# Gram blocks in groups of 32 tokens, two blocks in a row: a correlation stage beside attention

## The chip, the cores and the metric

The kernel runs on one NeuronCore of a Trainium2 chip. The metric is the device time of one execution in microseconds (us); the time given for a kernel is the median of three runs. One further execution is profiled, and everything that is read from a trace comes from that one.

The core has TensorE (PE, matrix products into PSUM; PEld is its weight loads), VectorE (DVE), ScalarE (ACT), GpSimd (POOL) and SyncE (SP), whose queue issues nearly all DMAs here. Each works through its own instructions in order and waits on semaphores for the others.

## The reference

The input is a batch of 8 images of 768 channels and 32 x 32 pixels. Two layers are computed in float32, with a group normalisation over 32 groups of channels ahead of each:

```python
x = x + _L0_conv_ref(_gn(x), L0_conv_W_qkv, L0_conv_W_proj, L0_conv_b_proj)
x = x + _L1_conv_ref(_gn(x), L1_conv_conv_w, L1_conv_conv_b)
```

The first layer is an attention over the 1024 pixels (tokens) with 12 heads of 64, whose scores come from the variances of keys and values alone:

```python
var_v = jnp.var(v, axis=-1, ddof=1, keepdims=True)
var_k = jnp.var(k, axis=-1, ddof=1, keepdims=True)
scores = var_v @ jnp.swapaxes(var_k, -2, -1) * scale
attn = jax.nn.softmax(scores, axis=-1)
out = attn @ v
```

Its result goes through a 768 x 768 projection. The second layer normalises every pixel's channel vector to length 1 and correlates it with 28 of its neighbours in a 7 x 7 window (the two diagonals, the middle column and the middle row), then mixes the 768 channels and the 28 correlations with a 1 x 1 convolution:

```python
norm = jnp.sqrt(jnp.sum(feature * feature, axis=1, keepdims=True))
feat_n = feature / jnp.maximum(norm, EPS)
feat_pad = jnp.pad(feat_n, ((0, 0), (0, 0), (PAD, PAD), (PAD, PAD)))
corr = jnp.stack([jnp.sum(feat_pad[:, :, r:h + r, cc:w + cc] * feat_n, axis=1) for r, cc in _offsets()], axis=1)
x = jnp.concatenate([feature, corr], axis=1)
out = jnp.einsum('bchw,oc->bohw', x, conv_w) + conv_b[None, :, None, None]
```

## The kernel before

**Layout.** Channels lie on the 128 partitions, six to each (`J = 6`), so an image is a tile of 128 x 6 x 1024. The large products (keys and values, projection, convolution) are done with Strassen's seven products; all of them have 64 columns of weights per matmul, two matmuls side by side in the two halves of the array (`halves`, L346 to L350). A float32 matmul stands in the trace as two records, one for each of its passes.

**Stages.** For image b a round of the main loop runs the keys and values of pairs 3 to 5 (half 1), the attention of its six pairs of heads (`Attention`, `Pair`), beside it the second layer's convolution of image b-1 (`Conv`), then the projection, then the keys and values of pairs 0 to 2 of image b+1. The work order is fixed when the program is built: a planner (`Clock`) holds a planned time, every unit of TensorE work advances it by a cost written down as a constant (`KV_US`, `T_US`, `STEP_US`, `GRAM_US`), and jobs for other engines are put behind it with `later.after(us, job)`, or `later.after_dve(us, job)`, which counts from the planned end of VectorE's work. These times only set the order of the instructions in each engine's queue; on the chip semaphores decide.

**The correlation of an image** (`Corr`). Only products of a pixel with pixels at up to 3 rows below and 3 columns to either side are needed. The 1024 tokens are cut into 8 blocks of four image rows (128 tokens). For each block t:

- `turn` (L1128) copies the block's tokens on GpSimd (ScalarE in the last image) so that the tokens of the left 16 columns come first and those of the right 16 after, two operations of 128 x 384 each, into the one buffer of `turnpool`.
- `gram` (L1143) multiplies, for each of the six channel chunks and for each side, the 64 tokens of that side (weights) with the part of the image they need: 7 rows (the block's four and three more) by 19 columns, 133 in all; the last block has 4 rows, 76. The two sides go to the two halves of the partitions in one PSUM tile of the pool `smp`, whose two banks are shared with other small products.
- `out` copies the result to one of three `wins` buffers (VectorE; ScalarE in the last image) and writes it with two DMAs to a DRAM area `windowed`, with a pitch between tokens such that a later read finds fixed neighbours at fixed places. After blocks 3 and 7 comes `diagonals` (L1182), which reads the 20 wanted products of each token of four blocks with four DMAs. `scale` (L1198) makes the inverse lengths (`rn`, a power on GpSimd) and multiplies; `to_dram` turns them into rows by two small matmuls (`ct`) and writes them to DRAM; after the second half `gather` (L1231) reads the rows into `cs` (u) and a tile of `uvpool` (v), each shifted by its offset, VectorE multiplies the two, and three DMAs copy `cs` to the other three quarters of the partitions. The convolution's units then add the correlations with one more matmul from `cs` (`join`, L1058).

**What places the Gram.** `work_off` (L1403) runs the attention's steps (four key tiles, 6.9 us) whenever their exponentials are made, and otherwise the next unit of the list `rest`. Gram units lie in a list of their own, `beside`: `next_to` (L1396) takes one of them before and after each attention step, and at two or three fixed places in `rest`; `remaining` takes what is left before the convolution starts. The first `turn` of an image is made when the keys and values of the next half are nearly done (`start_corr`); for image 0 it is made right after the normalisation (`turn_first`), and `"turned"` is released 6 us later.

**Other places that the change touches.** `KeysValues.unit` (L644) ends a half with `spread`, which reduces the variances, takes a maximum over partitions on GpSimd (`partition_all_reduce`, L714) and writes the rows that the attention reads. `make_sums` (L631) forms on GpSimd the token sums that the Strassen products of keys and values need. At the start `keep_warm` runs matmuls on an identity while the first data arrive.

Of the kernel before, what the change touches and what calls it, by code (L numbers as in the profile page):

```python
# [13 lines left out]
P = 128  # L14
# [15 lines left out]
TALL, WIDE = MT // 2 + 3, HW + 3  # L30
AHEAD_OF = [o for first, _, count in RUNS for o in range(first, first + count)][1:]
# [25 lines left out]
GRAM_US = 1.4  # L57
WARM, BRIDGE = 38, (3, 6)
# [33 lines left out]
class Clock:  # L92


    def __init__(self):
        self.now, self.count, self.jobs = 0.0, 0, []
        self.act, self.rows, self.poll = 0.0, ([], []), lambda: None
        self.dve = 0.0
# [74 lines left out]
def two_layers(ctx, tc, x, wkv, wproj, bproj, wconv, wcorr, bconv, out):  # L173
# [17 lines left out]
    turnpool = pool("turnpool", 1)  # L191
    wk = pool("wk", 3)
    uvpool = pool("uvpool", 1)
# [259 lines left out]
    wins = [const.tile([P, WIN], F32, name=f"win{i}") for i in range(3)]  # L453
# [141 lines left out]
    class KeysValues:  # L595
# [48 lines left out]
        def unit(self, half, d, n, g, p):  # L644
# [18 lines left out]
            if d == 1 and n == len(PAIR) - 1:  # L663
                self.over = half == 1
                more = 4.0 if half and not b else 0.0
# [458 lines left out]
    class Corr:  # L1124
# [17 lines left out]

        def gram(self, t):  # L1143

            b = self.b
            tall = min(TALL, H - 4 * t)
# [5 lines left out]
            for j in range(J):  # L1152
                image = self.f[:, j, :].rearrange("p (y x) -> p y x", x=W)
                for side in range(2):
                    left = side * (HW - 3)
                    nc.tensor.matmul(  # L1156
                        ps[side * HD : (side + 1) * HD, :n].rearrange("p (y x) -> p y x", x=WIDE),
                        lhsT=block[:, j, side, :],
                        rhs=image[:, 4 * t : 4 * t + tall, left : left + WIDE],
                        start=j == 0, stop=j == J - 1,  # L1160
                    )
            for ahead in range(t + 1, min(t + (3 if b == NB - 1 else 2), MT)):
# [3 lines left out]
            def out():  # L1166
                win = wins[t % 2 if t < MT - 1 else 2]
# [4 lines left out]
                for side in range(2):  # L1172
                    to = windowed[b % 2][t : t + 1, side * (HD * PITCH + HD - 3) :]
                    nc.sync.dma_start(
                        out=windows(to, (HW * PITCH - 3, 4), (PITCH, HW), (1, WIN)), in_=win[side * HD : (side + 1) * HD, :]
# [4 lines left out]
            later.after(GRAM_US + 0.25, out)  # L1180

        def diagonals(self, hf):  # L1182
# [13 lines left out]
            later.after(6.0, lambda: self.scale(hf, dd))  # L1196

        def scale(self, hf, dd):  # L1198
# [7 lines left out]
            def columns():  # L1206
# [4 lines left out]
                later.after_dve(0.7 if b else 5.0 if hf else 7.5, lambda: to_dram(dn))  # L1211
# [19 lines left out]
        def gather(self):  # L1231
# [3 lines left out]
            v = uvpool.tile([NCH, N], F32, tag="uv", name=f"v{b}")  # L1235
            nc.sync.dma_start(out=v[NS:NCH, :], in_=windows(r[0:1, PAD:], (0, NS + 4), (1, N)))
            nc.sync.dma_start(out=u[2 * NS : NCH, :], in_=windows(r[1:2, PAD:], (0, 4), (1, N)))
            for n, (first, apart) in enumerate(PICKED):
                k, row = 3 * n, 2 + AHEAD_OF.index(first)
                nc.sync.dma_start(out=u[k : k + 3, :], in_=windows(r[row : row + 1, PAD:], (apart * ROW, 3), (1, N)))  # L1240
                nc.sync.dma_start(out=v[k : k + 3, :], in_=windows(r[0:1, PAD + first :], (apart, 3), (1, N)))
# [150 lines left out]
    def remaining(beside):  # L1392
        while beside:
            next_to(beside)
# [250 lines left out]
```

## Time and profile before

| | us |
|---|---|
| median of three runs | 2574.16 |
| lowest and highest run | 2573.71, 2581.83 |
| profiled execution | 2576.79 |
| its span, first to last instruction | 2575.1 |
| TensorE's records of Gram, first seven images (L1156): 133 columns, 76 columns | 84.3, 8.2 |
| the same in the last image | 10.0, 1.0 |
| GpSimd's turned blocks (L1141), 112 operations | 110.7 |
| granted TensorE clock | 1.000 |

A line of a profile page gives an engine, the line of the code, the operation, the tiles it writes and reads and how often; times are in us unless marked ns. A record's busy time is not its cost: matmuls overlap their neighbours, so the cost of a group of them is the time from its first start to the first start of what follows. A timeline's columns are start, duration (to the end of the last one merged), engine, line, operation, output and inputs, shapes and count; in brackets stands the engine's idle time before, and what ended it. A line of the list of waits has the waiting engine, tile and line, what it waited for, the time in all, how often, and the longest one.

### The profile page before, as it was taken

To read this page: it belongs to the slowest core of one execution; us is meant where nothing else is said; L and a number is where in the kernel's file an instruction comes from. 1 tells how busy PE (TensorE), PEld (TensorE's weight loads), DVE (VectorE), ACT (ScalarE), POOL (GpSimd) and SP (SyncE) were. 2 spreads that over 40 slices of the span, in tenths; PEclk is the share of its full clock that TensorE was granted. 3 is DMA by queue.
4 is the path that set the end of the run, shared out by engine and by line. 5 is a ranking of instruction groups with operands and counts; after the bars stand their busy time and mean duration, and the time that the engine had idled before them with its cause. 6 is when DMAs were issued, how large, how long until landed. Compare 5 with 4: busy or idle time off the path is not lost.

```text
span 2575.1 us, 40595 instructions
## 1 busy us (share of the span) xinstructions
PE 2566.3 (100%) x14694; PEld 1246.2 (48%) x14694; DVE 1582.3 (61%) x4125; ACT 1417.5 (55%) x1972; POOL 422.4 (16%) x449
## 2 busy tenths in 40 slices
PE   9999999999999999999999999999999999999999
PEld 6545356334554347633476434664344333475333
DVE  6868735775447853478534785358853587535764
ACT  1497279811697217971179711897118971199610
POOL 4320130004300043000430003300133001331000
PEclk9999999999999999999999999999999999999999
DMA  8766366355563655636556365563655636445333
GB/s 293 293 220 229 102 212 186 120 198 170 185 190 116 198 168 178 205 98 206 169 176 202 97 212 169 168 204 100 218 166 174 207 107 218 151 158 167 119 109 109
DMA packets 331818, 448.56 MB, mean 174 GB/s; under 512 B 68431, under 2 KB 252623, under 8 KB 331619
## 3 DMA queue, kind: packets, MB, share of 16 engines
q1 hardware_dynamic: 329554, 442.62, 53.8%
q10 hardware_dynamic: 2064, 3.34, 0.4%
q8 instruction: 117, 1.92, 0.3%
q14 instruction: 83, 0.67, 0.1%
HBM read 376.70 MB, written 64.78 MB: 171 GB/s over the span
## 4 chain that ended last, share of the span: by engine, by line
PE 96%; DMA 2%; ACT 1%; DVE 1%; SPq 0%; issue 0%; POOL 0%; ACTq 0%; POOLq 0%; DVEq 0%
PE x L350 34%; PE av L801 25%; PE y L350 17%; PE z L350 10%; PE own L350 5%; PE gr L1156 3%; PE den L832 1%; ACT ex L775 1%; ACT junk L785 0%; DMA bk<-kdr 0%; DMA kv<-in_wkv_dram 0%; PE z L1062 0%; PE cc L1275 0%; PE y L1062 0%; DVE acc L167 0%
## 5 line engine op out<-in xcount | busy, mean ns | idle before, releaser
L775 ACT ACTIVATE ex<-bc,nk 128x1024 f32<-128x1024 f32 x768 | 826.9, 1139 | 382.4 <-DMA bc<-vdr 256.7
L801 PE MATMUL av<-ex,v 128*64 128x512 f32 x3072 | 699.8, 593 | 0.3 <-ACT ex L775 0.2
L801 PEld LDWEIGHTS av<-ex,v 128*64 128x64 f32 x3072 | 303.8, 137 | 355.3 <-issue 262.0
L785 ACT ACTIVATE junk<-bk,vm 128x1024 bf16<-128x1024 f32 x368 | 421.4, 1145 | 41.5 <-issue 17.8
L167 DVE TENSOR_TENSOR acc<-acc,ex 128x1024 f32<-128x1024 f32 x300 | 344.7, 1216 | 0.0
L350 PE MATMUL y<-kv,s 128*64 128x384 f32 x1488 | 265.6, 487 | 0.9 <-POOL s L636 0.9
L350 PE MATMUL x<-kv,xn 128*64 128x384 f32 x1512 | 261.4, 486 | 0.3 <-DMA kv<-in_wkv_dram 0.3
L350 PE MATMUL x<-kv,s 128*64 128x384 f32 x1488 | 256.2, 486 | 0.0
L229 ACT COPY kp<-x 128x384 f32<-128x384 f32 x28 | 13.4, 479 | 404.8 <-PE x L350 396.0
L350 PEld LDWEIGHTS x<-kv,xn 128*64 128x64 f32 x1512 | 134.2, 137 | 109.9 <-issue 83.9
L350 PEld LDWEIGHTS x<-kv,s 128*64 128x64 f32 x1488 | 131.6, 137 | 108.0 <-issue 87.1
L350 PEld LDWEIGHTS y<-kv,s 128*64 128x64 f32 x1488 | 130.1, 137 | 99.6 <-issue 75.3
L530 POOL TENSOR_TENSOR rstda<-vea,neghalf 128x1 f32<-128x1 f32 x8 | 4.8, 596 | 949.1 <-DVE vea L167 949.1
L1141 POOL TENSOR_TENSOR turn<-f,ones 128x384 f32<-128x384 f32 x112 | 110.7, 1010 | 242.1 <-PE gr L1156 182.2
L350 PE MATMUL z<-kv,xn 128*64 128x384 f32 x768 | 135.4, 486 | 0.0
L350 PE MATMUL x<-f,wt 128*64 128x512 f32 x504 | 120.0, 593 | 0.0
L167 DVE TENSOR_TENSOR v<-y,v 128x128 f32<-128x128 f32 x180 | 41.0, 283 | 124.1 <-PE y L350 124.1
L636 POOL TENSOR_TENSOR s<-xn 128x384 f32<-128x384 f32 x64 | 65.6, 1035 | 294.8 <-PE x L350 183.0
L167 DVE BATCH_NORM_STATS2 vbn<-v 128x6 f32<-128x64 f32 x720 | 101.7, 211 | 0.0
L167 DVE SCALAR_TENSOR_TENSOR xn<-x,bconv_sb,xn 128x512 f32<-128x512 f32 x63 | 46.5, 747 | 89.1 <-PE x L350 86.1
L229 ACT COPY acc<-li 32x256 f32<-32x256 f32 x128 | 51.6, 403 | 82.9 <-DVE li L167 81.5
L350 PEld LDWEIGHTS z<-kv,xn 128*64 128x64 f32 x768 | 72.6, 137 | 49.9 <-issue 36.0
(199 smaller groups left out, 3126.2 us busy)
## 6 DMA issues: line engine op xcount, KB each, us to landing
kv<-kvs SPq DMA_DIRECT2D x124, 576.0 KB
kv<-in_wkv_dram SPq DMA_DIRECT2D x95, 576.0 KB
bc<-vdr SPq DMA_DIRECT2D x96, 512.0 KB
f<-in_x_dram SPq DMA_DIRECT2D x48, 512.0 KB
bk<-kdr SPq DMA_DIRECT2D x46, 512.0 KB
x1d<-f SPq DMA_DIRECT2D x42, 512.0 KB
xn<-x1d SPq DMA_DIRECT2D x42, 512.0 KB
out_dram<-xn SPq DMA_DIRECT2D x82, 256.0 KB
```

Source lines behind the costliest of these rows:

```text
L167: return getattr(self.engine, name)(*args, **kw)
L229: nc.scalar.copy(to, at)
L350: nc.tensor.matmul(out[at], lhsT=lhsT[:, at], rhs=rhs, start=start, stop=stop, **kw)
L530: nc.gpsimd.tensor_tensor(self.rstd, ve, neghalf[:, 0:1], ALU.pow)
L636: nc.gpsimd.tensor_tensor(self.sums[g][:, 0], a[g][2], a[g][3], ALU.add)
L775: nc.scalar.activation(ex, self.bc[e], AF.Exp, scale=self.kv.nk[self.half][:, h, t : t + 1])
L785: nc.scalar.activation(junk, self.bk[e], AF.Exp, scale=self.kv.m2[self.half][:, h, t : t + 1], accum_out=self.sums[:, e, t : t + 1],)
L801: nc.tensor.matmul(self.av[hf][e * HD : (e + 1) * HD, :], lhsT=self.vt[:, t, e, :], rhs=exs[e][:, hf * HF : (hf + 1) * HF], start=t == 0, ...
L832: nc.tensor.matmul(den[at * 32 : (at + 1) * 32, :], lhsT=ones[:, 0:32], rhs=self.acc[e][:, hf * HF : (hf + 1) * HF], start=True, stop=True,)
L1141: nc.gpsimd.tensor_tensor(to[:, :, side], half, windows(ones, ones.ap[0], (0, J), (HW, 4), (1, HW)), ALU.mult)
L1156: nc.tensor.matmul(ps[side * HD : (side + 1) * HD, :n].rearrange("p (y x) -> p y x", x=WIDE), lhsT=block[:, j, side, :], rhs=image[:, 4 * ...
```

## The change

For all images but the last, each side's 64 tokens are divided into two groups of two image rows, so a block has four groups of 32 tokens. Each group is multiplied with five rows by 19 columns (95), or four rows in the last block (76), and goes to a quarter of the partitions. The windows of a block are written with four DMAs of 32 partitions (two in the last block). `grams` runs two blocks in a row and stands in `beside` in the place of `gram`; another pair is taken 5.8 us of planned time later at the earliest, but for `remaining`, which sets that aside. `turnpool` has two buffers, `turn` is made for two blocks ahead (two at the start of an image), and `v` of `gather` lies in two tiles of that pool in the place of `uvpool`. There are four `wins` buffers instead of three. The scaling of the diagonals is expected 13 us after their reads are issued instead of 6, and the rows' transposition at other times. The spread of image 0's half 1 is put 8 us later. Image 0's pairs of blocks have more places in `rest`, and `"turned"` is released 8 us after the first turned blocks. Four more matmuls stand in the first stretch of `keep_warm` and one more in a later one. The last image keeps two groups and single blocks.

```diff
--- before.py
+++ after.py
@@ -28,6 +28,7 @@
 RUNS = ((0, 0, 4), (31, -1, 3), (62, -2, 5), (93, -3, 7))
 HW = W // 2
 TALL, WIDE = MT // 2 + 3, HW + 3
+SHORT = 2 + 3
 AHEAD_OF = [o for first, _, count in RUNS for o in range(first, first + count)][1:]
 NA = len(AHEAD_OF)
 PAD = 99
@@ -54,8 +55,8 @@
 TAIL = 0.0
 EXP, SUM, STEP_US = 1.07, 1.15, 1.73
 KV_US, T_US, CORR_US = 1.93, 2.58, 1.2
-GRAM_US = 1.4
-WARM, BRIDGE = 38, (3, 6)
+GRAM_US, TURN_US = (1.3, 2.4), 3.4
+WARM, BRIDGE = 42, (3, 7)
 
 
 
@@ -95,7 +96,7 @@
     def __init__(self):
         self.now, self.count, self.jobs = 0.0, 0, []
         self.act, self.rows, self.poll = 0.0, ([], []), lambda: None
-        self.dve = 0.0
+        self.dve = self.turned = 0.0
 
     def after(self, us, job):
         self.count += 1
@@ -188,9 +189,8 @@
     bcpool = pool("bcpool", 4)
     bkpool = pool("bkpool", 2)
     expool = pool("expool", 2 * AHEAD)
-    turnpool = pool("turnpool", 1)
+    turnpool = pool("turnpool", 2)
     wk = pool("wk", 3)
-    uvpool = pool("uvpool", 1)
     st = pool("st", 1)
     xbank = pool("xbank", 2, space=PSUM)
     ybank = pool("ybank", 2, space=PSUM)
@@ -450,7 +450,7 @@
 
     rows = [dconst.tile([NROW, ROW], F32, name=f"rows{i}") for i in range(2)]
     windowed = [dconst.tile([MT, P * (PITCH + 2)], F32, name=f"windowed{i}") for i in range(2)]
-    wins = [const.tile([P, WIN], F32, name=f"win{i}") for i in range(3)]
+    wins = [const.tile([P, WIN], F32, name=f"win{i}") for i in range(4)]
     for win in wins:
         nc.gpsimd.memset(win, 0.0)
     across = const.tile([W, NA], F32, name="across")
@@ -662,7 +662,7 @@
                 kv_stream.done((b, half, d, p))
             if d == 1 and n == len(PAIR) - 1:
                 self.over = half == 1
-                more = 4.0 if half and not b else 0.0
+                more = 12.0 if half and not b else 0.0
                 later.after(KV_US + 0.5 + more, lambda: later.after_dve(0.0, lambda: self.spread(half)))
 
         def stats(self, kind, half, t, src):
@@ -1140,10 +1140,18 @@
                     half = rows[:, :, :, side, :]
                     nc.gpsimd.tensor_tensor(to[:, :, side], half, windows(ones, ones.ap[0], (0, J), (HW, 4), (1, HW)), ALU.mult)
 
+        def grams(self, t):
+
+            clock.turned = clock.now + GRAM_US[1] + TURN_US
+            for n in range(2):
+                self.gram(t + n)
+
         def gram(self, t):
 
             b = self.b
-            tall = min(TALL, H - 4 * t)
+            last = t == MT - 1
+            groups = 2 if b == NB - 1 else 4
+            tall = min(SHORT if groups == 4 else TALL, H - 4 * t)
             n = tall * WIDE
             if t not in self.turned:
                 self.turn(t)
@@ -1151,33 +1159,39 @@
             ps = other([P, SPAN], f"gr{b}_{t}")
             for j in range(J):
                 image = self.f[:, j, :].rearrange("p (y x) -> p y x", x=W)
-                for side in range(2):
-                    left = side * (HW - 3)
+                each = P // groups
+                for at in range(groups):
+                    side, low = divmod(at, groups // 2)
+                    left, first = side * (HW - 3), 4 * t + (0 if last else 2 * low)
                     nc.tensor.matmul(
-                        ps[side * HD : (side + 1) * HD, :n].rearrange("p (y x) -> p y x", x=WIDE),
-                        lhsT=block[:, j, side, :],
-                        rhs=image[:, 4 * t : 4 * t + tall, left : left + WIDE],
+                        ps[at * each : (at + 1) * each, :n].rearrange("p (y x) -> p y x", x=WIDE),
+                        lhsT=block[:, j, side, low * each : (low + 1) * each],
+                        rhs=image[:, first : first + tall, left : left + WIDE],
                         start=j == 0, stop=j == J - 1,
                     )
-            for ahead in range(t + 1, min(t + (3 if b == NB - 1 else 2), MT)):
+            for ahead in range(t + 1, min(t + 3, MT)):
                 if ahead not in self.turned:
                     self.turn(ahead)
 
             def out():
-                win = wins[t % 2 if t < MT - 1 else 2]
+                win = wins[t % 3 if t < MT - 1 else 3]
                 if b < NB - 1:
                     vector.tensor_copy(win[:, :n], ps[:, :n])
                 else:
                     act_copy(0.3, win[:, :n], ps[:, :n])
-                for side in range(2):
-                    to = windowed[b % 2][t : t + 1, side * (HD * PITCH + HD - 3) :]
+                whole = last or groups == 2
+                size, count, down = (WIN, 4, 0) if whole else (SHORT * WIDE + 3, 2, 2 * (HW * PITCH - 3 + WIDE))
+                for first in range(0, P, count * HW):
+                    side, low = divmod(first, HD)
+                    to = windowed[b % 2][t : t + 1, side * (HD * PITCH + HD - 3) + (down if low else 0) :]
                     nc.sync.dma_start(
-                        out=windows(to, (HW * PITCH - 3, 4), (PITCH, HW), (1, WIN)), in_=win[side * HD : (side + 1) * HD, :]
+                        out=windows(to, (HW * PITCH - 3, count), (PITCH, HW), (1, size)),
+                        in_=win[first : first + count * HW, :size],
                     )
                 if t % 4 == 3:
                     later.after(4.0, lambda: self.diagonals(t // 4))
 
-            later.after(GRAM_US + 0.25, out)
+            later.after(1.65 if b == NB - 1 else GRAM_US[t % 2] + 0.25, out)
 
         def diagonals(self, hf):
 
@@ -1193,7 +1207,7 @@
                     ),
                 )
                 at += count
-            later.after(6.0, lambda: self.scale(hf, dd))
+            later.after(13.0 if b < NB - 1 else 6.0, lambda: self.scale(hf, dd))
 
         def scale(self, hf, dd):
 
@@ -1208,7 +1222,7 @@
                 vector.tensor_copy(dn[:, :, 0], rn)
                 for q in range(4):
                     vector.scalar_tensor_tensor(dn[:, q, 1:NROW], dd[:, q, :], rn[:, q : q + 1], mask, ALU.mult, ALU.mult)
-                later.after_dve(0.7 if b else 5.0 if hf else 7.5, lambda: to_dram(dn))
+                later.after_dve(0.7 if b == NB - 1 else (5.0 if hf else 7.0) if b else 3.0 if hf else 6.0, lambda: to_dram(dn))
 
             def to_dram(dn):
                 pt = small(f"ct{b}_{hf}")
@@ -1232,20 +1246,23 @@
 
             b, r = self.b, rows[self.b % 2]
             u = cs.rearrange("p a n -> p (a n)")[0:NCH, 0:N]
-            v = uvpool.tile([NCH, N], F32, tag="uv", name=f"v{b}")
-            nc.sync.dma_start(out=v[NS:NCH, :], in_=windows(r[0:1, PAD:], (0, NS + 4), (1, N)))
+            vs = [turnpool.tile([P, J * P], F32, tag="turn", name=f"v{b}_{hf}") for hf in range(2)]
+            for hf, v in enumerate(vs):
+                nc.sync.dma_start(out=v[NS:NCH, :HF], in_=windows(r[0:1, PAD + hf * HF :], (0, NS + 4), (1, HF)))
             nc.sync.dma_start(out=u[2 * NS : NCH, :], in_=windows(r[1:2, PAD:], (0, 4), (1, N)))
             for n, (first, apart) in enumerate(PICKED):
                 k, row = 3 * n, 2 + AHEAD_OF.index(first)
                 nc.sync.dma_start(out=u[k : k + 3, :], in_=windows(r[row : row + 1, PAD:], (apart * ROW, 3), (1, N)))
-                nc.sync.dma_start(out=v[k : k + 3, :], in_=windows(r[0:1, PAD + first :], (apart, 3), (1, N)))
+                for hf, v in enumerate(vs):
+                    nc.sync.dma_start(out=v[k : k + 3, :HF], in_=windows(r[0:1, PAD + first + hf * HF :], (apart, 3), (1, HF)))
                 nc.sync.dma_start(
                     out=u[NS + k : NS + k + 3, :],
                     in_=windows(r[row : row + 1, PAD - first :], (apart * (ROW - 1), 3), (1, N)),
                 )
 
             def product():
-                vector.tensor_tensor(u, u, v, ALU.mult)
+                for hf, v in enumerate(vs):
+                    vector.tensor_tensor(cs[0:NCH, hf, :], cs[0:NCH, hf, :], v[0:NCH, :HF], ALU.mult)
                 vector.tensor_tensor(cs[0:NCH, 2, :], cs[0:NCH, 0, :], cs[0:NCH, 1, :], ALU.subtract)
                 for n in range(1, 4):
                     nc.sync.dma_start(out=cs[n * FOUR : n * FOUR + NCH, :, :], in_=cs[0:NCH, :, :])
@@ -1391,11 +1408,12 @@
 
     def remaining(beside):
         while beside:
+            clock.turned = 0.0
             next_to(beside)
 
     def next_to(beside):
 
-        if beside and ready.issuperset(beside[0][1]):
+        if beside and ready.issuperset(beside[0][1]) and clock.now >= clock.turned:
             us, _, unit = beside.pop(0)
             unit()
             clock.pass_time(us)
@@ -1421,7 +1439,7 @@
 
     def turn_first():
         start_corr(0)
-        later.after(6.0, lambda: ready.add("turned"))
+        later.after(8.0, lambda: ready.add("turned"))
 
     def project(b, ots, held=None):
         f = first_f[0] if b == 0 else layer1[b - 1][0]
@@ -1538,6 +1556,7 @@
     def start_corr(b):
         corrs.append(Corr(b, layer1[b][0]))
         corrs[-1].turn(0)
+        corrs[-1].turn(1)
 
     second, corrs = [], []
     later.after(26.0, lambda: sum_weights(1, 9.0, 1.5))
@@ -1570,11 +1589,15 @@
                         later.after(1.5 * n, lambda n=n: nc.sync.dma_start(out=f[:, n, :], in_=xv[b, :, n, :]))
 
                 conv.then = low_residual
-            grams = [(GRAM_US if t < MT - 1 else 0.9, has_f if b > 1 else has_f + ("turned",), lambda t=t: (corr or corrs[0]).gram(t)) for t in range(MT)]
+            if b < NB:
+                keys = has_f if b > 1 else has_f + ("turned",)
+                grams = [(GRAM_US[1], keys, lambda t=t: (corr or corrs[0]).grams(t)) for t in range(0, MT, 2)]
+            else:
+                grams = [(1.4 if t < MT - 1 else 0.9, has_f, lambda t=t: corr.gram(t)) for t in range(MT)]
             first, start = (0.0, has_f, conv.sums.first), (0.0, (), conv.start)
             if b < NB:
                 beside = grams
-                for n in (3, 7) if b > 1 else (7, 11, 15):
+                for n in (3, 7) if b > 1 else (7,) + tuple(range(12, 30, 2)):
                     rest.insert(n, (0.0, has_f, lambda: next_to(beside)))
                 rest.insert(len(rest) - 4, (0.0, has_f, lambda: remaining(beside)))
                 rest.insert(len(rest) - 4, first)
```

## The prediction

> **What bounds the kernel now.** I read the page's first part, its chain and the list of who waited for whom on TensorE, then the TensorE timeline around the Gram blocks, in that order.
>
> ```profile
> span 2575.1 us, 40595 instructions
> PE 2566.3 (100%) x14694; PEld 1246.2 (48%) x14694; DVE 1582.3 (61%) x4125; ACT 1417.5 (55%) x1972; POOL 422.4 (16%) x449
> ...
> PE 96%; DMA 2%; ACT 1%; DVE 1%; SPq 0%; issue 0%; POOL 0%; ACTq 0%; POOLq 0%; DVEq 0%
> ```
>
> ```profile
> PE y L350 <- POOL s L636: 0.9, 1, 0.9
> PE pma L350 <- DVE mva L167: 0.8, 1, 0.8
> PE gr L1156 <- POOL turn L1141: 0.5, 2, 0.2
> PE gr L1156 <- ACT win L229: 0.4, 2, 0.2
> ```
>
> TensorE is the bound everywhere: the chain is 96% its own, and its listed waits are single short ones. So only two things can move the time: how long the Gram matmuls hold TensorE, and waits added to or taken from it. What other engines save is worth nothing by itself.
>
> **The Gram's price now.** Two stretches of the TensorE timeline, one for a block of 133 columns and one for the last block of an image (76):
>
> ```profile
> 652.66 1.53 PE L1156 MATMUL gr<-f,turn 128*64 128x133 f32 x24
> 654.02 2.10 PE L350 MATMUL y<-kv,s 128*64 128x384 f32 x12
> ...
> 712.03 1.02 PE L1156 MATMUL gr<-f,turn 128*64 128x76 f32 x24
> 712.82 2.48 PE L350 MATMUL x<-kv,s 128*64 128x384 f32 x14
> ```
>
> The second column overlaps with what follows, so I take start to start: 1.36 us and 0.79 us. A block has 12 matmuls (6 chunks, 2 sides), each two records, and both sides run side by side in their halves of the array: 12 steps, 0.113 us each at 133 columns and 0.066 us at 76. From these two rows a column costs (1.36 - 0.79) / 57 = 0.010 us per block. The first seven images have 49 blocks of 1.36 and 7 of 0.79: 72.2 us.
>
> **After, per block.** Four groups of 32 tokens, each against 5 rows of 19 = 95 columns. If the four run side by side as the two did, the steps stay 12 and a block costs 0.79 + 19 x 0.010 = 0.98 us: 0.38 less. The last block keeps 76 columns (4 rows). 49 x 0.38 = **18.6 us saved**. The last image keeps two groups.
>
> **The price of the narrower columns.** The kernel has one other place with 32-wide weights, the denominators:
>
> ```profile
> 248.45 4.05 PE L350 MATMUL z<-kv,xn 128*64 128x384 f32 x24
> 252.43 1.07 PE L832 MATMUL den<-acc,ones 128*32 128x512 f32 x8
> 253.43 2.80 PE L801 MATMUL av<-ex,v 128*64 128x512 f32 x12
> ```
>
> Going in: 24 records of this shape take 3.87 us undisturbed (the same row in the chain), so the next should start at 252.32; it starts at 252.43: 0.11. Inside and out: two passes of 512 columns are 0.86 us at the rate of the attention matmuls (32 records, 16 passes, in 6.87); here 1.00: 0.14. The first matmul after such a stop is 51 ns longer (Gram durations: median 277 ns, longest 328): 0.05. Together 0.30 us per excursion. Two blocks in a row share one: 4 per image, 28 in seven images: **8.4 us paid**. Bounds: 0.2 (no inner cost) to 0.45 (the extra start paid in each block), 5.6 to 12.6 us.
>
> **Rate of records, the one thing the trace does not show.** A step now starts four records, 0.98 / 48 = 20 ns apart, for 96 records on end. In the trace four 32-wide records start within 0.02 us, but the densest longer run is the 24 records in 0.79 us: 33 ns. [...]
>
> **Order of the work.** (a) Image 0's spread of pairs 3 to 5 goes 8 us later, behind the token sums.
>
> ```profile
> 150.23 0.44 POOL L714 PARTITION_ALL_REDUCE most<-top  x1 [11.55 <-DVE top L167]
> 157.59 2.47 POOL L636 TENSOR_TENSOR s<-xn 128x384 f32<-128x384 f32 x2 [6.92 <-DVE rsv L167]
> ```
>
> GpSimd stands 6.92 us after the all-reduce before it makes the sums (after the one at 1603.44 it stands 7.92), and TensorE's y waits 0.9 for them. With the sums first that goes: **0.9 saved**. What is late instead: the sums' 8 operations end about 162, the all-reduce follows some 7 us later, and VectorE's scaling of the keys, which waits for it, holds the copies out of PSUM queued behind it until about 170. TensorE is then at 168.0 and reads no freed bank before about 172: I take 0, at most 2. SP's rows for pair 3 (issued 172.55) move 4 to 8 us; their exponentials start at 190.96, so they are covered; without cover, up to 8.
>
> (b) Two turned blocks are kept ahead instead of one. In image 0 the two waits for turn (0.5) go, since the first unit now starts with both made (its release is 2 us later). For the second unit I checked the tightest place:
>
> ```profile
> 1603.44 0.44 POOL L714 PARTITION_ALL_REDUCE most<-top  x1 [7.40 <-DVE top L167]
> 1611.80 1.97 POOL L1141 TENSOR_TENSOR turn<-f,ones 128x384 f32<-128x384 f32 x2 [7.92 <-PE x L350]
> ```
>
> There the first block starts at 1606.37; two blocks and three products (3 x 1.93) later is 1614.5, so the fourth block comes at 1615.6, and its tile is done at 1611.80 + 2 x 1.97 = 1615.7. Late by 0.1 to 0.5 in some images, as the second block is now (1613.5 against 1613.77). Net 0; at worst 0.5 x 7. Later units are at least 5.8 us apart and two tiles take 3.9. **0.5 saved.**
>
> (c) A fourth win buffer: the last image's two waits of Gram for the win copy (0.4), which wait for the write of a buffer two blocks back, go. **0.4 saved.**
>
> (d) Per image 14 more writes on SP (0.5 us each, under the two rows of windows each block had) and 5 more gathers (0.27 each, in the last image 1.4 us later for the product); diagonals' scaling 7 us later, the transposed columns up to 4.3 us later. Cover: the last Gram block comes some 25 us earlier (four units, 8 to 9 us apart, instead of eight), and the correlation is copied at 759.4 while its first matmul is at 778.9. In the last image the copies end about 2553 and the first use is at 2557.2. So 0. [...]
>
> (e) Four more warm matmuls (8 records, 0.11 each, 0.9 us) fall in the 0.79 us in which pma waits anyway, and one more bridge (0.22) in the 0.35 before x: 0 to 0.1. Memset of a win, the split of the product into two operations, smaller win copies: on POOL and VectorE, hidden under TensorE.
>
> **Sum.** -18.6 + 8.4 - 0.9 - 0.5 - 0.4 = **-12.0 us**. The profiled execution took 2576.79 (span 2575.1 and 1.7 around it), so it would be 2564.8, with a span of 2563.1. The median of the runs is 2574.16 (2573.71 to 2581.83), 2.6 below the profiled one; on it: **2562.2**, 0.47% faster. A change under 0.3% (7.7 us) can't be told from none here.
>
> **Rivals.**
> Waits in new places (chance 0.15): the turned tiles late in each image's second unit (0.5 x 7 = 3.5), VectorE held behind image 0's all-reduce (2), PSUM's two shared banks both taken by a pair of blocks when VectorE is behind (0.3 in some images): 5 to 8 us given back, 2567 to 2570. For it: the 1615.6 against 1615.7. Against: VectorE is busy 31.4 of the 80 us from 640 to 720.
> [...]
> Slower, by one mechanism (0.09): records enter the array no faster than the trace's densest run, 33 ns, since each of the four groups needs its own weight load and matmul from one queue. 56 x 1.58 = 88.5 against 72.2, + 8.4 - 1.8: +22.9, 2597. It decides from 24.4 ns on: 56 x 48 x r = 72.2 - 8.4 + 1.8 gives the break-even. Against: the four den records 7 ns apart.
> The change as summed: 0.65.
>
> **Range and chances.** The likeliest alone: excursion bounds and hidden waits give 2558 to 2567. The range of 8 in 10 takes in the new waits and the floor: 2557 to 2579; what is left out is the 33 ns case and beyond, and some of each side. Faster by over 0.3% (below 2566.4): 0.63 of the sum's 0.65, a fifth of the new waits: 0.66. Within 0.3%: most of the rest of the waits and of the floor: 0.20. Slower: 0.14.
>
> **What would show it.** Gram blocks 0.98 us start to start with 48 records each, 2.2 to 2.3 us for a pair with its way in and out, about 0.3 us lost per pair at its edges; no y waiting for POOL s at 159; the 28 pairs adding no rows to TensorE's list of waits. Wrong if a pair takes 2.7 us or more (records too slow), or if gr waits for turn grow beyond 3 us.

## The result and the profile after

The changed kernel takes **2598.69 us** (median of 6 runs, 2594.49 to 2603.76) against 2576.94 (2573.71 to 2581.83) for the kernel before in the same comparison: ratio 1.0081, 95% interval 1.0071 to 1.0091. It is 0.8% slower where 0.5% faster was forecast. The profiled executions took 2599.55 and 2576.79, 22.8 us apart.

The head of the page and the chain by engine, after:

```profile
span 2597.8 us, 43513 instructions
PE 2574.9 (99%) x16048; PEld 1140.4 (44%) x16048; DVE 1593.2 (61%) x4133; ACT 1415.7 (54%) x1972; POOL 422.1 (16%) x450
...
PE 90%; ACT 4%; issue 2%; DMA 2%; DVE 2%; SPq 0%; ACTq 0%; DVEq 0%
```

The busy shares hardly moved; the chain did, from 96% TensorE to 90%, with 4% of ScalarE. TensorE's list of waits, after (engine, line, who it waited for: total, times, longest):

```profile
PE av L801 <- ACT ex L775: 16.1, 12, 3.1
PE warm L419 <- POOL ident masks.py:199: 1.6, 1, 1.6
PE x L350 <- DVE t2o L168: 0.6, 1, 0.6
PE pma L350 <- DVE mva L168: 0.4, 1, 0.4
```

The waits that the prediction expected to go (y for the token sums, Gram for its turned tiles, Gram for the win copies) are gone. In their place the attention products wait 16.1 us for exponentials; before, that line was 0.2.

The Gram itself does what was promised. TensorE timeline after, image 2, first pair of blocks:

```profile
971.52 2.11 PE L350 MATMUL y<-kv,s 128*64 128x384 f32 x12
973.55 2.17 PE L1166 MATMUL gr<-f,turn 128*32 128x95 f32 x96
975.65 2.16 PE L350 MATMUL y<-kv,s 128*64 128x384 f32 x12
```

From the first start of the pair to the next start of y, 96 records and the way out take 2.10 us. With the way in (0.10 us ahead of the first start) and a longer first matmul behind (0.05) a pair takes 2.25, inside the 2.2 to 2.3 of the prediction.

To see the rest I charged each matmul record the spacing at which its shape runs undisturbed (0.429 us per pass of 512 columns, from 16 passes in 6.87 us; 0.322 for 384, 12 in 3.87; 0.113, 0.082 and 0.066 for 133, 95 and 76), and summed what of the array's time was left over, by the matmul ahead of which it was lost:

```
us                    before   after
Gram work             82.5     63.9    -18.6
lost ahead of gr       3.5      6.3     +2.8
lost ahead of y        4.8      9.8     +5.0
lost ahead of x        3.1      4.0     +0.9
lost ahead of av      10.3     42.7    +32.4
```

These five lines make +22.5 of the 22.8. They are estimates: how the gaps at the borders of groups are charged moves a line by some 3 us (with every gap charged to the next pass, av comes to +35 and the three lines above it to +6). One line was not in my sum at all: the 32 to 35 us of av.

**Where they come from.** The stretch around the first attention products of image 3. SP's timeline after (start, us, then line, what it issues, how many), from the maximum over the keys on GpSimd, which starts at 970.53:

```profile
976.39 1.84 SPq L764 DMA_DIRECT2D bc<-vdr  x2
978.33 2.53 SPq L1187 DMA_DIRECT2D windowed<-win  x4
980.90 4.30 SPq L593 DMA_DIRECT2D kdr<-rsk  x2
985.31 2.51 SPq L1187 DMA_DIRECT2D windowed<-win  x4
987.93 0.93 SPq L306 DMA_DIRECT2D kv<-in_wkv_dram  x2
988.90 2.76 SPq L1187 DMA_DIRECT2D windowed<-win  x4
991.71 0.97 SPq L764 DMA_DIRECT2D bk<-kdr  x2
```

And before, where the maximum starts at 966.83:

```profile
973.69 1.09 SPq L1174 DMA_DIRECT2D windowed<-win  x2
974.88 5.48 SPq L593 DMA_DIRECT2D kdr<-rsk  x2
980.41 1.00 SPq L306 DMA_DIRECT2D kv<-in_wkv_dram  x2
981.50 1.09 SPq L1174 DMA_DIRECT2D windowed<-win  x2
982.65 1.18 SPq L764 DMA_DIRECT2D bk<-kdr  x2
```

`bk` is the key row that the softmax's denominators need. 12 window writes of some 0.63 us each stand ahead of it instead of 4 of 0.55, so it is issued 21.2 us after the maximum instead of 15.8. The other images from 2 to 7 show the same: 19.8 to 21.4 us in all six, before 15.5 to 17.1. The rows themselves are no slower: from their issue to the first denominator it is 5.9 us after, 6.7 before. ScalarE's timeline after shows who waits for them:

```profile
982.64 5.31 ACT L775 ACTIVATE ex<-bc,nk 128x1024 f32<-128x1024 f32 x5 [0.16 <-DMA bc<-vdr]
997.56 1.15 ACT L785 ACTIVATE junk<-bk,vm 128x1024 bf16<-128x1024 f32 x1 [9.61 <-issue]
998.61 0.19 ACT L785 ACTIVATION_READ_ACCUMULATOR junk<-bk,vm 128x1 f32 x1
998.70 4.25 ACT L775 ACTIVATE ex<-bc,nk 128x1024 f32<-128x1024 f32 x4
```

`junk` is the first denominator. ScalarE stands 9.61 us ahead of it, and the exponentials of steps 3 and 4, which need nothing of `bk`, stand behind it. TensorE's timeline, same place:

```profile
991.79 5.37 PE L801 MATMUL av<-ex,v 128*64 128x512 f32 x24
999.89 3.86 PE L801 MATMUL av<-ex,v 128*64 128x512 f32 x8 [2.73 <-ACT ex L775]
```

Three steps run, then TensorE waits for the fourth's exponentials. The profile names no releaser for ScalarE's 9.61 us ("issue"); that it is bk is an inference here, and the run with the writes alone, below, names it. Before, ScalarE stood ahead of the first denominator too:

```profile
989.33 1.15 ACT L785 ACTIVATE junk<-bk,vm 128x1024 bf16<-128x1024 f32 x1 [5.54 <-issue]
990.39 0.19 ACT L785 ACTIVATION_READ_ACCUMULATOR junk<-bk,vm 128x1 f32 x1
990.48 4.25 ACT L775 ACTIVATE ex<-bc,nk 128x1024 f32<-128x1024 f32 x4
```

That is 22.5 us after the maximum (27.0 after the change). The first exponential behind it ended at 991.61 and av's fourth step began at 992.53, so av ran without a stop with 0.9 us to spare. After the change the denominator is 4.5 us later and av itself starts 0.7 later: 4.5 - 0.7 - 0.9 leaves 2.9 us, and av's next start comes 2.9 us late (999.89 instead of 996.99). So the kernel before had this wait with nearly all of its slack used.

### The profile page after: what moved, and what is told of

It is laid out like the page before. It is cut to its first block, busy times and chain, and to the rows that moved or that the text cites. A ratio compares the mean times of both kernels' runs of the same rounds, so it can differ in the third digit from the quotient of the medians.

```text
span 2597.8 us, 43513 instructions
## 1 busy us (share of the span) xinstructions
PE 2574.9 (99%) x16048; PEld 1140.4 (44%) x16048; DVE 1593.2 (61%) x4133; ACT 1415.7 (54%) x1972; POOL 422.1 (16%) x450
## 4 chain that ended last, share of the span: by engine, by line
PE 90%; ACT 4%; issue 2%; DMA 2%; DVE 2%; SPq 0%; ACTq 0%; DVEq 0%
PE x L350 33%; PE av L801 22%; PE y L350 16%; PE z L350 10%; PE own L350 5%; ACT ex L775 3%; PE gr L1166 2%; ACT junk L785 1%; PE den L832 1%; DMA bc<-vdr 1%; DVE acc L168 0%; DMA xn<-in_x_dram 0%; DVE v L168 0%; PE y L1062 0%; PE z L1062 0%
## 5 line engine op out<-in xcount | busy, mean ns | idle before, releaser
L801 PE MATMUL av<-ex,v 128*64 128x512 f32 x3072 | 734.7, 596 | 16.4 <-ACT ex L775 16.1
L801 PEld LDWEIGHTS av<-ex,v 128*64 128x64 f32 x3072 | 264.0, 137 | 438.1 <-issue 338.9
L350 PE MATMUL y<-kv,s 128*64 128x384 f32 x1488 | 276.2, 488 | 0.0
L350 PE MATMUL x<-kv,xn 128*64 128x384 f32 x1512 | 273.0, 486 | 0.0
L350 PE MATMUL x<-kv,s 128*64 128x384 f32 x1488 | 264.3, 486 | 0.0
L350 PE MATMUL x<-f,wt 128*64 128x512 f32 x504 | 134.0, 592 | 0.0
```

What stands on the lines that cost most here:

```text
L350: nc.tensor.matmul(out[at], lhsT=lhsT[:, at], rhs=rhs, start=start, stop=stop, **kw)
L801: nc.tensor.matmul(self.av[hf][e * HD : (e + 1) * HD, :], lhsT=self.vt[:, t, e, :], rhs=exs[e][:, hf * HF : (hf + 1) * HF], start=t == 0, ...
```

## The experiments

**Theories.** *Queue*: the added window writes on SP delay bk, the first denominators with it, and on ScalarE, which works in order, the exponentials behind them. *Pairing*: two blocks in a row displace the products, or the planner's order of the attention, whatever SP does. *Buffers*: three rotating win buffers hold VectorE's copies until the writes have landed, and VectorE holds the keys' scaling. Medians below are beside 2576.6 to 2577.0 for the kernel before in the same comparisons.

### Window writes later

```diff
-    wins = [const.tile([P, WIN], F32, name=f"win{i}") for i in range(4)]
+    wins = [const.tile([P, WIN], F32, name=f"win{i}") for i in range(5)]
...
-                win = wins[t % 3 if t < MT - 1 else 3]
+                win = wins[t % 4 if t < MT - 1 else 4]
...
+                later.after(12.0 if b < NB - 1 and t < 4 else 0.0, lambda: write(win))
+
+            def write(win):
```

> The changed kernel, with the window writes of each image's first four blocks (seven images) issued 12 us of planned time later, so that none of the 12 stands on SP's queue ahead of the first pair's bk rows (and a fifth win buffer to hold the windows meanwhile). Queue theory (writes ahead of bk make the first denominators late, the exponentials behind them on ScalarE late, and TensorE's av wait): the first denominators start about 20 us after the keys' all-reduce instead of 27, the 16 us of av waiting for ex and the half-clock stretches behind it go, some 32 us in all; 2567, between 2562 and 2573. Pairing theory (two blocks in a row push the products so that the exponentials are late by themselves): the av waits stay, 2596 to 2601. Buffer theory (win copies wait for the writes of a buffer and hold VectorE): the buffers are held longer here, so 2599 or more.

**2573.46 us**, ratio 0.9987 (0.9981 to 0.9994). SP's timeline now has no window write between the keys' rows and bk:

```profile
972.75 4.94 SPq L593 DMA_DIRECT2D kdr<-rsk  x2
977.79 0.96 SPq L306 DMA_DIRECT2D kv<-in_wkv_dram  x2
978.80 1.12 SPq L764 DMA_DIRECT2D bk<-kdr  x2
979.97 1.05 SPq L764 DMA_DIRECT2D bc<-vdr  x2
981.06 11.04 SPq L1190 DMA_DIRECT2D windowed<-win  x9
```

bk comes 12.9 us after the maximum (965.90), the first denominator 20.7 after it, and the av waits for exponentials fall from 16.1 to 0.9. What is lost ahead of av falls from 42.7 to 16.7. The buffer theory, which asked for more waiting here, is out, and so is pairing as the main cause. But I expected 2567 (2562 to 2573), and some 6 us of the av loss were still there: a second cause.

### More win buffers alone

```diff
-    wins = [const.tile([P, WIN], F32, name=f"win{i}") for i in range(4)]
+    wins = [const.tile([P, WIN], F32, name=f"win{i}") for i in range(5)]
...
-                win = wins[t % 3 if t < MT - 1 else 3]
+                win = wins[t % 4 if t < MT - 1 else 4]
```

> The changed kernel with four rotating win buffers instead of three, nothing else. Buffer theory (VectorE's window copy stands until a buffer's write has landed, and what is behind it on VectorE, the keys' scaling among it, comes late): the waits of win for windowed go, 2575 to 2590. Queue theory: the 12 writes still stand ahead of bk, 2597 to 2601. Pairing theory: 2597 to 2601.

**2595.65 us**, ratio 1.0070 (1.0054 to 1.0087). Three us less than the changed kernel, with intervals that overlap; bk still 21.3 us after the maximum, av still waiting (10.6 us listed). Buffers are not the cause, at most a small part.

### Two writes per block

```diff
-                whole = last or groups == 2
+                whole = True
```

> The changed kernel with two window writes of 64 partitions per block instead of four of 32, in the layout of the kernel before (the correlation's diagonals of half of the tokens are then read from wrong places; every other operation is there). 6 writes stand ahead of bk instead of 12, 6 x 0.6 = 3.6 us less of the 5.4 us. Queue theory: most of the av waits go, 2567 to 2580. Pairing theory and buffer theory: 2594 to 2601.

**2582.74 us**, ratio 1.0022 (1.0014 to 1.0030). bk 17.3 us after the maximum, 3.9 earlier than in the changed kernel; av waits 3.4 us. 16 of the 22 us come back with half the number of writes and no fewer bytes, so the number of issues counts. The diagonals of half of the tokens are then read from wrong places, by the same operations. The time is slightly above the range of the queue theory (2567 to 2580): bk is still 1.5 us later than before, and the second cause is in this run too.

### The writes alone, in the kernel before

```diff
-                for side in range(2):
-                    to = windowed[b % 2][t : t + 1, side * (HD * PITCH + HD - 3) :]
+                count = 1 if b < NB - 1 and t < 2 else 4
+                for first in range(0, P, count * HW):
+                    side, low = divmod(first, HD)
+                    to = windowed[b % 2][t : t + 1, side * (HD * PITCH + HD - 3) + low // HW * (HW * PITCH - 3) :]
...
-                        out=windows(to, (HW * PITCH - 3, 4), (PITCH, HW), (1, WIN)), in_=win[side * HD : (side + 1) * HD, :]
+                        out=windows(to, (HW * PITCH - 3, count), (PITCH, HW), (1, WIN)), in_=win[first : first + count * HW, :]
```

`count` is the number of 16-partition pieces in a DMA: blocks 0 and 1 are written by eight DMAs each.

> The kernel before, single blocks of two groups, where only the windows of each image's first two blocks (seven images) are written by eight writes of 16 partitions instead of two of 64: 16 writes stand ahead of bk instead of 4, 12 x 0.5 = 6 us more, same output. Queue theory: the first denominators come about 6 us later and av waits for ex in each image as in the changed kernel, 20 to 40 us more: 2597 to 2617. Pairing theory and buffer theory: no pair of blocks and no third buffer here, 2575 to 2580.

**2595.28 us**, ratio 1.0074 (1.0059 to 1.0089): 18.5 us slower from 12 more DMAs per image, with no split of the Gram and no pairs. bk comes 21.0 us after the maximum (988.86 against 967.91). TensorE's waits:

```profile
PE av L801 <- ACT ex L775: 12.8, 8, 2.9
PE warm L419 <- POOL ident masks.py:199: 1.6, 1, 1.6
```

And ScalarE's first denominator in image 3, now with its releaser:

```profile
993.20 1.15 ACT L785 ACTIVATE junk<-bk,vm 128x1024 bf16<-128x1024 f32 x1 [8.67 <-DMA bk<-kdr]
```

This makes the loss from the suspected cause alone. It fell a little short of the 20 to 40 expected.

### The writes on GpSimd's queue

```diff
-                    nc.sync.dma_start(
+                    (nc.sync if b == NB - 1 else nc.gpsimd).dma_start(
```

> The changed kernel with the window writes of seven images issued by GpSimd instead of SP, at the same place in the order of work. Queue theory in its narrow form (what delays bk is the time that SP spends on issuing each write): bk is issued about 16 us after the keys' all-reduce, the av waits go, 2567 to 2578, the upper end if GpSimd's turned tiles come late behind the writes. If instead the writes' transfers delay bk's landing (or the copies' waits on VectorE do it), the place of issue is indifferent: 2594 to 2601.

**2606.80 us**, ratio 1.0115 (1.0098 to 1.0132), outside every range that I gave. The listed waits on TensorE:

```profile
PE ct L353 <- DVE dn L168: 17.8, 7, 2.8
PE av L801 <- ACT ex L775: 3.5, 2, 1.9
PE gr L1166 <- DVE win L168: 3.4, 5, 1.4
```

Taken apart, the queue theory holds: the same writes at the same place delay bk no more (12.4 us after the maximum), and av waits 3.5 instead of 16.1. But GpSimd's queue has work behind the writes too. Its timeline in image 3:

```profile
1009.22 2.35 POOL L1187 DMA_DIRECT2D windowed<-win  x4 [0.44 <-DVE v L168]
1011.59 1.08 POOL L1218 TENSOR_TENSOR rn<-m,neghalf 128x4 f32<-128x4 f32 x1
```

And VectorE's in the same run, just after:

```profile
1012.70 0.57 DVE L168 COPY dn<-rn 128x4 f32<-128x4 f32 x1 [3.20 <-POOL rn L1218]
1013.08 8.87 DVE L168 SCALAR_TENSOR_TENSOR dn<-dd,rn,mask 128x19 f32<-128x19 f32 x4
```

The diagonals' inverse lengths (`rn`) come after the writes, the scaled columns (`dn`) later still, and the two small matmuls (`ct`), which stand in TensorE's queue at a fixed place, wait for them seven times, up to 2.8 us. In the changed kernel `rn` started at 1005.41 instead of 1011.59, and the four `dn` took 3.95 us instead of 8.87:

```profile
1009.33 3.95 DVE L168 SCALAR_TENSOR_TENSOR dn<-dd,rn,mask 128x19 f32<-128x19 f32 x4
```

So two things make the new stall, `rn` behind the writes and slower operations after it; no run separates them. The stall was moved, not removed: writes were put ahead of work on another queue without a look at who waits for it.

### Exponentials ahead of the first denominator

```diff
-                    SUM, lambda: pair.rows_at.get(("k", e)), lambda: self.denominators(pair, t, e), 1
+                    SUM, lambda: self.may_sum(pair, e), lambda: self.denominators(pair, t, e), 1
+        def may_sum(self, pair, e):
+            at = pair.rows_at.get(("k", e))
+            if self.b > 0 and pair.hp == 0 and e == 0 and at is not None and clock.now + 1.0 < at:
+                return None
+            return at
...
-            first = {(1, "c"): 10.5, (1, "k"): 10.5, (2, "k"): 9.0}.get((min(self.b, 2), kind), 9.0)
+            first = {(1, "c"): 10.5, (1, "k"): 10.5, (2, "k"): 12.0}.get((min(self.b, 2), kind), 9.0)
```

> The changed kernel with all 12 writes ahead of bk as they are, but with each image's first denominator (images 2 on, six of them) put behind the exponentials of steps 3 and 4 on ScalarE instead of ahead of them. Queue theory, second link (late rows hurt only because ScalarE works in order and a denominator that waits for them stands ahead of exponentials that don't need them): bk stays as late, the av waits for ex go nearly all, 2570 to 2576, with the 0.7 us in five images left in. If the exponentials themselves come late (their rows, their buffers, pairs of blocks), or the wait only moves to the next denominator, 2590 to 2600.

**2566.90 us**, ratio 0.9961 (0.9947 to 0.9975): 31.8 us less than the changed kernel, and faster than the kernel before. This settles the second link. SP issues as in the changed kernel, and bk is nearly as late (984.99, 19.8 us after the maximum at 965.15). ScalarE's order is what differs:

```profile
988.62 4.27 ACT L775 ACTIVATE ex<-bc,nk 128x1024 f32<-128x1024 f32 x4 [6.19 <-PE av L801]
992.79 1.13 ACT L785 ACTIVATE junk<-bk,vm 128x1024 bf16<-128x1024 f32 x1
```

The first denominator starts 27.6 us after the maximum, no earlier than in the changed kernel (27.0), and delays nobody, because the exponentials of steps 3 and 4 are ahead of it. Not all of the 31.8 is this link, as the second cause, below, goes in this run as well. The late row was harmless; a waiting instruction ahead of others that were urgent was not.

### The second cause

In the run with late writes av lost 0.7 us in each of five images, about 8 us behind the correlation's matmuls, and 0.5 more some 20 us later. VectorE's timeline there:

```profile
805.17 0.68 DVE L168 TENSOR_TENSOR xn<-z,xn 128x512 f32<-128x512 f32 x1
805.77 1.22 DVE L168 TENSOR_TENSOR v<-v,rd 128x1024 f32<-128x1024 f32 x1
806.90 2.35 DVE L168 TENSOR_TENSOR acc<-ex,ex 128x1024 f32<-128x1024 f32 x2
```

The third pair's product of values by inverse sums stands ahead of the sums of exponentials that free ScalarE's buffers. Before, it stood ahead of the idle time (799.39, while the `xn` operations came at 805.30). The change didn't touch it; its new planned costs moved the planner's times by a few us, and that swapped it with the output operations. Planned 2 us earlier:

```diff
-            self.rd_at = clock.now + {HP // 2: 8.0, HP - 2: 12.0}.get(self.hp, 14.0)
+            self.rd_at = clock.now + {HP // 2: 8.0, HP - 2: 12.0, 2: 12.0}.get(self.hp, 14.0)
```

> The run with late writes, with the product of the third pair's values by their inverse sums (v by rd on VectorE) planned 2 us earlier. In the changed kernel it has slipped behind four operations of the convolution's output and holds the sums of exponentials, and so the exponentials and av, by 0.7 us in each of five images. If that is the cause of these: 2573.5 - 3.5 = 2570, between 2568.5 and 2571.5. If not, 2573 to 2574.

**2567.83 us**, ratio 0.9965 (0.9952 to 0.9978), 5.6 less than with late writes alone, where 3.5 was expected (only the 0.7 had been counted); the product is back at 798.00. In the run with the exponentials first, the swap goes by itself (the product comes after the sums, at 808.43), and the same edit on top should then do little:

> The run with the exponentials first, with the third pair's product of v by rd planned 2 us earlier as well. If the two causes add (late denominators, and the product that slipped on VectorE), some 5 us less than the run with the exponentials first, 2565 to 2571, as with late writes. If the order of ScalarE has removed the slip's effect already, no more than 1 us less.

**2566.55 us**, ratio 0.9958 (0.9943 to 0.9973): 0.35 less, as the second of the two cases. This is the fastest version, 10.1 us (0.4%) below the kernel before. With the second cause out of both, the two ways of mending the first (2567.83 with late writes, 2566.55 with the exponentials first) are 1.3 us apart, with intervals that overlap.

### The Gram's split by itself, and image 0

```diff
-            groups = 2 if b == NB - 1 else 4
+            groups = 2
```

> The run with late writes (2573.5), with its Gram in two groups of 64 tokens and 133 columns again; pairs of blocks, late writes, image 0's order and all else stay. The Gram's split by itself: 18.6 us of matmul time come back and the 28 ways in and out of the 32-wide weights (about 8.5 us) go, so if the split is worth what the prediction's sum says, 2573.5 + 10.1 = 2583.6, between 2580 and 2587. If the split's gain is eaten at the edges (an excursion of 0.6 us instead of 0.3), 2573 to 2576.

**2581.73 us**, ratio 1.0019 (1.0011 to 1.0026). Undone, the split costs 8.3 us, so its net worth is 8.3 where the prediction's two terms give 10.2. The edit also gives a block two window writes again instead of four; they stand behind bk in both runs, and what is lost ahead of av differs by about 1 us.

```diff
-                more = 12.0 if half and not b else 0.0
+                more = 4.0 if half and not b else 0.0
```

> The run with late writes, with image 0's spread of pairs 3 to 5 ahead of the next keys' token sums again, as in the kernel before. The prediction's step (a): y waits 0.9 us for the sums on GpSimd again and nothing else changes, 2574.4. If the later spread costs what it saves (av stood 0.4 to 0.5 us at 180 us in the kernels with it), 2573 to 2574.

**2574.47 us** against 2573.46 with late writes alone, 1.0 more, and TensorE's list has its old line back:

```profile
PE y L350 <- POOL s L636: 0.9, 1, 0.9
```

The difference of the medians is within their spread; the line is what shows the wait. But the later spread has a price of its own, which I had put at 0: with it, av loses 0.45, 0.32 and 0.32 us in image 0 (at 182.55, 199.79 and 210.53), in the kernel before and in this run less than 0.05 at each of these places. That is 1.1 us against the 0.9 saved; the last av of image 0 starts at 268.85 with the late spread and at 269.15 with the early one. So this step was worth at most some 0.3 us.

## Why the prediction was wrong

**What bounds the kernel.** Right as a reading of the chain, and not enough. "Its listed waits are single short ones" tells that nothing waits, not by how much. ScalarE stood 5.54 us ahead of the first denominator before, and I did not look at how little was left behind it.

**The Gram, -18.6.** Right: 82.5 to 63.9. The rate of records, which the trace of before didn't show, was decided rightly. A pair's 96 records in 2.10 us are 21.9 ns each with the way out; at 33 ns, the densest longer run in the trace of before, they would take 3.17. The range and the chances also count in a floor under the records' spacing; no run shows the term, and what the changed kernel shows in its place is these 21.9 ns. The slower rival gave 2597, close to the result, by a mechanism that did not happen.

**The ways in and out, +8.4.** Right in size. From the last pass ahead of a pair to the second one behind it, less the undisturbed spacing, an excursion costs 0.28 us in 25 of the 28 pairs of the fastest version, where 0.30 was forecast: 7.8 us for 28. In the run with late writes 23 pairs lose 0.28 and five, three of them in image 0, lose 0.49 to 1.56, which makes 10.5; the run with the split undone gives 18.6 - 8.3 = 10.3. So the price of the narrower columns was right, and the remainder is waits at a few pairs.

**(a), (b), (c), -1.8.** The waits named are gone from the list, and y's 0.9 comes back when the spread of image 0 is put back. But (a) took the lateness of that spread as hidden ("I take 0, at most 2"), and av pays 1.1 for it, so of the 1.8 some 0.7 were left. None of the waits that I feared for the turned tiles appears in the changed kernel's list.

**(d), 0: the step that failed.** It says "Per image 14 more writes on SP (0.5 us each ...)" and covers them with the correlation's own slack, 19 us between the copies of cs and their first use. That slack was there. But the writes delayed what was queued behind them on SP, whoever needed that, and the bk rows were behind them: 12 writes instead of 4, 5.4 us. I named no work that stood behind the writes. In place of the 0, the runs show some 18.5 us for the writes alone in the kernel before; in the changed kernel, 25 us go when they are moved. With ScalarE's order changed 31.8 go, of which some 5 are the slip of the next paragraph.

**Slips in the planner's order.** Costed at 0 as well. By the run that puts it back, 5.6 us came from an operation that no line of the diff names.

**The sum.** -18.6 + 8.7 + 32.4 make 22.5 (the small waits that went are in the 8.7, the sum of the lines of gr, y and x), against 22.8 measured. Without the 32.4 the change would have been worth about 10 us, and the two repaired versions measure 9.7 and 10.1 of the 12.0 forecast. The rest is in av: 12.2 us are lost there in the fastest version against 10.3 before. Image 0's later spread is 1.1 of these 1.9; the cause of what is left was not looked for.

**What I said would make it wrong** (a pair of 2.7 us, Gram waiting for turn) did not come about. The list held only dangers at the place of the change; the damage was on two other engines' queues.

## What to carry to other kernels

The added DMAs were priced here by what stood behind them on their queue (12 more writes per image in the kernel before put bk 21.0 us behind the maximum in image 3 instead of 15.8, and cost 18.5 us in all), not by whether their own data came in time: list the instructions behind, and follow each to who waits for it. Where an in-order engine has an instruction that waits for late data, put the urgent work that doesn't need them ahead of it: that was worth as much here as making the data earlier (2566.55 and 2567.83 us). And when costs in a planned order are changed, compare the whole order of every engine: here an operation far from the edit changed places, for 5.6 us.

## What was not expected of the hardware

**TensorE's clock was halved after two stalls of the changed kernel, and the length of a stall alone does not decide it.** Five stretches of the changed kernel, four around the wait of image 3 and one with the wait of image 7 (us, engines' busy times, then the granted clock, the DMA share and GB/s):

```profile
985.00:996.50 11.50, 11.50 (x148) 5.46 (x146) 4.74 (x29) 2.95 (x3) 5.82 (x6) 1.00 0.63 205
996.50:999.80 3.30, 0.66 (x4) 0.00 (x0) 0.02 (x1) 2.24 (x4) 0.00 (x0) 0.93 0.83 307
999.80:1001.00 1.20, 1.11 (x3) 0.36 (x5) 0.00 (x0) 1.20 (x3) 0.00 (x0) 0.50 0.12 46
1001.00:1003.40 2.40, 2.40 (x8) 0.80 (x6) 0.00 (x0) 2.40 (x3) 0.00 (x0) 0.63 0.08 18
2284.00:2292.00 8.00, 5.08 (x104) 2.38 (x104) 0.33 (x2) 6.95 (x9) 0.00 (x0) 1.00 0.40 146
```

In image 3 no matmul starts for 3.3 us (996.56 to 999.89; the listed wait is 2.73), and the clock is granted at half for about 3.4 us (3.3 x 0.07 x 2 + 1.2 + 2.4 x 0.37 x 2). The same happened in image 5, after a wait of 3.08 us (granted 0.86 from 1640 to 1652). But the wait of image 7, 2.92 us and so longer than that of image 3, was followed by the full clock. In the trace's record of the clock the two half stretches last 3.413 us each and begin 645.12 us apart, which is 189.0 times 3.413. What decides, beside the length of a stall, is not shown by these runs. The price: from the first av pass after the stall to the next pair of Gram blocks it takes 2.90 us in images 2 and 7 at the full clock, and 3.79 and 4.10 in images 3 and 5 at the half one, so some 2 of the 32.4 us.

**VectorE's scaled columns beside GpSimd.** The change puts some of the 64 small operations `dn` next to GpSimd's token sums. They take 583 ns in the mean instead of 234, 33.5 us in all instead of 10.9, and 59.4 with the window writes on GpSimd, where four of them took 8.87 us (above). In image 3 the four beside the sums take 3.95 us and the next four, with GpSimd idle, 0.68. That the sums are what slows them is an inference from this; no run here isolates it, nor shows by what it would come. In the changed kernel nobody waited for them; on GpSimd's queue ct did.
